# Order of the sync queue, the place of the mask bias, and the order on ScalarE in a graph-attention kernel

## The chip, the cores and the metric

The kernel runs on one core of one Trainium2 chip. The metric is the device time of one execution in microseconds (us), the median over the runs shown. One core has a matrix engine (TensorE, PE in the profile; its weight loads stand on a line of their own, PEld), three engines that work on tiles in on-chip memory (VectorE = DVE, ScalarE = ACT, GpSimd = POOL), and SyncE (SP), which here does nothing but start transfers between main memory and on-chip memory. Each engine runs its own list of instructions strictly in order. An instruction that waits for another engine or for a transfer holds up everything behind it on its own list; that includes SP, whose list is called the sync queue here.

## The reference

Sixteen sequences (B = 16) of N = 512 positions and F = 512 features; 16 heads; every position attends to the first 20 positions only, in two directions with their own weights. Cut to what matters:

```python
def _forward(v, q, adj, W_self, b_self, w_bias, b_bias, Wq, bq, Wk, bk, Wout, bout):
    row_zero = v.sum(-1) == 0
    q_exp = jnp.where(row_zero[..., None], 0.0, q[:, None, :])
    self_feat = jnp.concatenate([v, q_exp], axis=-1) @ W_self.T + b_self
    output = self_feat
    for d in range(2):
        A = adj_f if d == 0 else jnp.swapaxes(adj_f, 1, 2)
        A = A[:, :, :20, :]                       # (B, 512, 20, 11)
        cond, vb = A.sum(-1), A @ w_bias + b_bias
        # inside _gat_attention:
        aff = jnp.einsum('bnhd,bmhd->bnhm', qh, kh) / sqrt(dh)
        aff = jnp.where(cond[:, :, None, :] > 0, aff, -9e15) + vb[:, :, None, :]
        w = softmax(aff)                          # over the 20 keys
        output = output + einsum(w @ kv, Wout) + bout
    return v + relu(output)
```

Two details carry the change. `row_zero` is a flag for each position, and `q` is added only where the row's sum is not zero. `b_bias` is one number that is added to every attention score.

## The kernel before

**Setup.** Weights and key-side products that don't depend on the 512 query positions are made first: keys `g` (for each sequence a 128 x 4 x 608 tile; the first in `g0`, the second stored to `g1_d`, the others to `g_d`), the score terms from the biases `cq` (stored to `cq_d`, L524), values `vw` (stored to `vw_d`). In the main part values are read back in a block layout: `clear_blocks` (L123) writes zeros over all of `bd_d` (2 MB), `blocks` (L130) copies the values into it with 12 transfers, `load_values` (L115) loads one sequence's blocks into `vd` with four transfers.

**Main loops.** For each sequence b (16) there are four steps nt (tiles of 128 query positions). The order of all instructions is written out by hand: the scheduler is off (`manual_schedule`), so an engine's list is the order in which the Python calls are made. The names for each step:

- `store()` at the start of each step sends the finished output tiles to memory (256 KB each, four for each sequence). What `residual` (L337) has appended by then is sent.
- `load_adj(b, h)` the mask of half a sequence (440 KB, three buffers); `load_cq` four transfers; `load_x` (1 MB, four buffers); `load_xn` two halves of the sequence in another layout (512 KB each, one buffer for each half), which serve only the row sums; `load_keys` (1.2 MB, two buffers); `load_values` (four transfers, **one** buffer, so a new load must wait until `attend` of the sequence before has read the old one).
- `self_feat(b, f, h)` on TensorE (L186) makes half of the feature rows for half of the positions into a PSUM bank; `self_copy` (L194, the vector instruction at L199) adds `q` times the row flag `nz` and moves it to `sf`. For sequence b+1, `ahead` puts (f 0 and 1, h 0) into step 3 of sequence b, and (0, 1) and (1, 1) into its own steps 0 and 1.
- `scores` on TensorE (L253, 128 matmul instructions as the profile counts them) needs `sf` and the keys. `weigh` on VectorE (L267, L271, L273), `expo` on ScalarE (L278), `normal` (L304, L305 on VectorE, L306 on GpSimd) and `turn` (L313 on VectorE) make the softmax; `normal` and `turn` of a step stand one step later.
- `attend(b - 1)` on TensorE (L324) stands in step 2 of sequence b and writes four PSUM banks, which it shares with `self_feat` (`ps_acc` has four). `finish` (L333 on VectorE, the relus at L335 on ScalarE) takes them out.
- The mask: `mask_mul` casts the integers on ScalarE (L207) and multiplies by the weights on GpSimd (L208); `mask_count` (L213 on VectorE, L214 on GpSimd) adds the large negative number; `mask_sum` reduces (L219 on VectorE); `mask_spread` copies the result to the 128 partitions with 16 small instructions on ScalarE (L228), which also add `b_bias` (`bb_sb`); `full_add` (L242 on GpSimd) adds `cq`.

**The row flags.** `row_sum` (L149, ScalarE, four for each sequence) sums the rows of `xn`. `row_mask` (L151) turns the sums into flags on VectorE (L153) and sends 2 KB to memory (`nz_d`, L154). `load_nz` (L156) loads them back, spread over all partitions (`nz`, L158); it has to wait until the store has landed. For b = 0 and 1 the flags are made on chip in the setup; the other 14 sequences go through memory.

**The sync queue for one sequence before**, in order: [step 1] mask half 0 of b+1, `cq` of b+1; [step 2] values of b, keys of b+1, x of b+2, mask half 1 of b+1, both halves of `xn` of b+2, flags of b+1 to memory, flags of b+1 back; [steps 3 and 0] four outputs. For b = 0 the clearing and the 12 block copies stand in step 1, ahead of x(2) and of mask half (1, 1).

Of the kernel before, what the change touches and what calls it, by code (L numbers as in the profile page):

```python
# [9 lines left out]
AF = mybir.ActivationFunctionType  # L10
# [3 lines left out]
P = 128  # L14
# [4 lines left out]
def gat_kernel(  # L19
# [20 lines left out]
    nc = tc.nc  # L40
    B, F, N = xT.shape
# [5 lines left out]
    BM = B * NG  # L47
# [4 lines left out]
    R = P // HL  # L52
# [39 lines left out]
    def load_xn(b, h):  # L92
        t = xns[b, h] = load.tile([P, 2, F], F32, tag="xn", name=f"xn{b}_{h}")
        nc.sync.dma_start(t, xn[b].rearrange("(p j) f -> p j f", j=4)[:, 2 * h : 2 * h + 2])
# [15 lines left out]
    def load_keys(b):  # L110
        gs[b] = gp.tile([P, C, WD], F32, tag="g", name=f"g{b}")
        src = g1_d if b == 1 else g_d[:, :, b - 2]
        nc.sync.dma_start(gs[b].rearrange("p c (a w) -> p (c a) w", a=C), src.rearrange("x p w -> p x w"))

    def load_values(b):  # L115

        vds[b] = gp.tile([P, HL, 2, DH], F32, tag="vd", name=f"vd{b}", bufs=1)
        for c in range(C):
            nc.sync.dma_start(
                vds[b][bass.ts(c, 32)].rearrange("p e i g -> p (e i g)"), bd_d[c, b].rearrange("r e i g -> r (e i g)")  # L120
            )
# [8 lines left out]
    def blocks():  # L130

        bb = bd_d.rearrange("c b r e i g -> (c b) r e i g")
        vv = vw_d.rearrange("d c (b m) (e g) -> d (c b) m e g", m=NG, e=HL)
        for e in range(HL):
            for i in range(2):
                j = (e * S) // 32 + i
                for d in range(2):
                    lo = max(e * S + d * NG, 32 * j)
                    hi = min(e * S + (d + 1) * NG, 32 * j + 32)
                    if lo < hi:  # L140
                        m, r = lo - e * S - d * NG, lo - 32 * j
                        nc.sync.dma_start(bb[:, r : r + hi - lo, e, i], vv[d, :, m : m + hi - lo, e])  # L142
# [8 lines left out]
    def row_mask(b, queue=nc.sync):  # L151
        t = msk.tile([P, 4], F32, tag="nz4", name=f"nz4_{b}")
        nc.vector.tensor_scalar(t, rss[b], 0.0, None, ALU.not_equal)  # L153
        queue.dma_start(nz_d[b].rearrange("(p j) -> p j", j=4), t)  # L154

    def load_nz(b, queue=nc.sync):  # L156
        nzs[b] = load.tile([P, N], F32, tag="nz", name=f"nz{b}")
        queue.dma_start(nzs[b], nz_d[b : b + 1].partition_broadcast(P))  # L158
# [45 lines left out]
    def mask_mul(b, h):  # L204
        a = adjs[b, h]
        p = prods[b, h] = msk.tile([P, 2 * S, L + 1], F32, tag="prod", name=f"prod{b}_{h}", bufs=1)
        nc.scalar.copy(p[:, :, :L], a.rearrange("p t (m l) -> p (t m) l", l=L))  # L207
        nc.gpsimd.tensor_mul(p[:, :, :L], p[:, :, :L], wb_sb.unsqueeze(1).to_broadcast([P, 2 * S, L]))  # L208
# [13 lines left out]
    def mask_spread(b, h, quarters=range(4)):  # L222

        add = conds[b, h]
        for a in quarters:
            for g in range(HL):
                r = bass.ts(g, R)
                nc.scalar.activation(  # L228
                    adds[b, h][bass.ts(a, R), :, g], add[r].rearrange("p (t m) -> p t m", t=2),
                    AF.Identity, bias=bb_sb[r],  # L230
                )

    def mask_add(b, h):
        mask_sum(b, h)
        mask_spread(b, h)
# [111 lines left out]
    with tc.tile_pool(name="setup", bufs=1) as sp:  # L347
# [157 lines left out]
        with tc.tile_pool(name="setup_g", bufs=4) as sg:  # L505

            def bias_scores(d):

                ps = ps_acc.tile([P, 512], F32, tag="acc", name=f"ps_c{d}")
                for c in range(C):  # L510
                    nc.tensor.matmul(
                        ps[bass.ts(c, DH), : B * ND], bqbd[:, d, c], khD[:, d * C + c],
                        start=True, stop=True,
                    )
                if d == 0:
                    stages["c"] = load.tile([P, 2, F], F32, tag="xn", name="c")
                    nc.gpsimd.memset(stages["c"][:, :, :BM], 0.0)
                t = stages["c"][:, d, :BM]
                nc.scalar.copy(
                    t.rearrange("p (b m) -> p b m", m=NG)[:, :, 1:],  # L520
                    ps[:, : B * ND].rearrange("p (b m) -> p b m", m=ND),
                )
                for c in range(C):
                    nc.gpsimd.dma_start(  # L524
                        cq_d[:, bass.ts(c, HL), d].rearrange("b h m -> h b m"),
                        t[c * DH : c * DH + HL].rearrange("p (b m) -> p b m", m=NG),
                    )
# [130 lines left out]
    with tc.manual_schedule():  # L658
# [11 lines left out]
        for b in range(B):  # L670
# [13 lines left out]
            for nt in range(NT):  # L684
                store()
                if nt == 1:
                    if b + 1 < B:
                        load_adj(b + 1, 0)
                        load_cq(b + 1)
                    if b == 0:  # L690
                        clear_blocks(zero)
                        blocks()
                if nt == 3 and b == 0:
                    load_values(b)
                if nt == 2:
                    if b > 0:
                        load_values(b)
                    if 0 < b < B - 1:
                        load_keys(b + 1)
                    if b + 2 < B:  # L700
                        load_x(b + 2)
                    if b + 1 < B:
                        load_adj(b + 1, 1)
                    if b + 2 < B:
                        load_xn(b + 2, 0)
                        load_xn(b + 2, 1)

                if b == B - 1 and nt == 2:

# [2 lines left out]
                    mask_add(b, 1)  # L712
                if nt == 3 and b + 1 < B:
                    mask_add(b + 1, 0)
                if prev is not None and (nt != 2 or b == 0):
                    normal(*prev)
                final = b == B - 1 and nt == NT - 1
# [7 lines left out]
                if nt == 2 and b > 0:  # L725
                    banks = [ps_acc.tile([P, 512], F32, tag="acc", name=f"ps_o{b - 1}_{q}") for q in range(4)]
                    attend(b - 1, banks)
                    o = work.tile([P, C, N], F32, tag="o", name=f"o{b - 1}")
                    finish(b - 1, o, banks)
                    normal(*prev)  # L730
                    if b + 1 in rss:
                        row_mask(b + 1)
                        load_nz(b + 1)
                if final:

                    o_last = gp.tile([P, C, WD], F32, tag="g", name=f"o{b}")[:, :, :N]
# [10 lines left out]
                    mask_mul(b, 1)  # L747
                    mask_count(b, 1)
                if nt == 2 and b + 1 < B:
                    mask_mul(b + 1, 0)  # L750
                    mask_count(b + 1, 0)
                for part in ahead(nt):
                    self_copy(*part)
# [30 lines left out]
                if nt >= 2 and b > 0:  # L784
                    if not final:
                        residual(b - 1, 2 * nt - 4, o)
                    residual(b - 1, 2 * nt - 3, o)
                if 0 < b < B - 1 and nt < 2:
                    row_sum(b + 1, 2 * nt)
                    row_sum(b + 1, 2 * nt + 1)  # L790
                prev = (b, nt, s)
        store()
        b = B - 1
# [80 lines left out]
```

## Time and profile before

| | value |
|---|---|
| median of 3 runs (lowest, highest) | 663.02 us (661.27, 664.54) |
| the profiled execution, own time | 666.13 us |
| its span in the trace | 664.3 us |
| mean granted TensorE clock | 0.983 |
| PE busy | 627.7 us, 94% |
| PEld busy | 462.0 us, 70% |
| DVE busy | 468.4 us, 71% |
| ACT busy | 362.7 us, 55% |
| POOL busy | 370.7 us, 56% |
| share of the last-ending chain that is PE | 85% |
| moved by transfers | 124.17 MB, mean 187 GB/s |

A line of the profile names the engine, the source line, the operation, the tile written and the tiles read. Busy time is the time in which an engine worked, idle time is given with what ended it. The chain of waits is followed back from the last instruction: at each step to what released it, or to the instruction before it on the same engine. "issue" is time in which an engine waited for nothing that the profile names. The granted clock is the share of the full TensorE clock.

### The profile page before, as it was taken

The page shows a single profiled execution, that of the slowest core. Times are in us where ns is not written, and L with a number is a line of the kernel's source. Part 1 is how long each engine was busy: PE and PEld are TensorE (multiplying, and loading weights), DVE is VectorE, ACT ScalarE, POOL GpSimd, SP SyncE. Part 2 cuts the span into 40 slices and gives each one's busy share as a digit, 9 for nine tenths or more (in the row PEclk, how much of TensorE's full clock was granted, in tenths as well). Part 3 has the DMA queues.
Part 4 walks back from the last instruction along what each step waited for, and adds up shares of the span by engine and source line. Part 5 has one row for each costly group of instructions (what it writes and reads, how often), then busy time and mean ns, then how long its engine had stood idle before and what let it go on. Part 6 is the DMA issues. An engine that isn't in the chain of part 4 may idle for free.

```text
span 664.3 us, 31036 instructions
## 1 busy us (share of the span) xinstructions
PE 627.7 (94%) x13932; PEld 462.0 (70%) x13932; DVE 468.4 (71%) x754; ACT 362.7 (55%) x862; POOL 370.7 (56%) x301
## 2 busy tenths in 40 slices
PE   9999999989989999898989899999989898999995
PEld 6654468847767768776777686686767677777883
DVE  1576658484949596785949494968768585949786
ACT  1335626274755647373847466473737384747671
POOL 3307225256574756565555757466655655575785
PEclk9999999979999999998999999999999999999998
DMA  8999997837171727364362717273736446362403
GB/s 302 389 381 312 368 326 212 238 95 263 30 275 56 263 87 239 114 221 133 110 244 72 249 42 273 75 242 112 238 116 209 146 145 209 85 243 57 150 29 127
DMA packets 97684, 124.17 MB, mean 187 GB/s; under 512 B 19504, under 2 KB 69712, under 8 KB 95504
## 3 DMA queue, kind: packets, MB, share of 16 engines
q1 hardware_dynamic: 96304, 120.31, 53.3%
q8 instruction: 109, 1.79, 1.1%
q0 software_dynamic: 672, 1.36, 0.9%
q10 hardware_dynamic: 576, 0.53, 0.3%
q14 instruction: 23, 0.19, 0.1%
HBM read 82.30 MB, written 40.24 MB: 184 GB/s over the span
## 4 chain that ended last, share of the span: by engine, by line
PE 85%; issue 5%; DMA 3%; DVE 3%; SPq 3%; ACT 0%; POOL 0%; DVEq 0%; POOLq 0%; ACTq 0%
PE ps_s L253 37%; PE ps_sf L186 30%; PE ps_o L324 7%; PE ps_v L537 3%; PE ps_k L475 3%; PE ps_kv L426 2%; SPq L142 2%; DMA bd_d<-zero 1%; DMA adj<-in_adj 1%; DMA g_d<-st 1%; PE ps_warm L385 1%; SPq L98 0%; DVE ps_s L271 0%; DVE wt L313 0%; DVE o L333 0%
## 5 line engine op out<-in xcount | busy, mean ns | idle before, releaser
L253 PE MATMUL ps_s<-g,sf 128*32 128x152 f32 x8192 | 286.8, 297 | 22.0 <-issue 21.5
L253 PEld LDWEIGHTS ps_s<-g,sf 128*32 128x32 f32 x8192 | 261.6, 111 | 57.2 <-issue 41.7
L186 PE MATMUL ps_sf<-x,ws_v 128*32 128x236 f32 (+1 forms) x4096 | 225.5, 371 | 1.8 <-issue 1.8
L228 ACT ACTIVATE both<-add,bb_sb 32x80 f32<-32x80 f32 x512 | 183.2, 358 | 42.6 <-DVE add L219 36.5
L186 PEld LDWEIGHTS ps_sf<-x,ws_v 128*32 128x32 f32 x4096 | 138.5, 110 | 72.0 <-issue 6.5
L242 POOL TENSOR_TENSOR full<-cq,both 128x640 f32<-128x640 f32 x64 | 99.9, 1562 | 92.5 <-ACT both L228 61.0
L278 ACT ACTIVATE s<-s 128x640 f32<-128x640 f32 x63 | 46.5, 738 | 180.6 <-DVE s L273 178.3
L306 POOL TENSOR_TENSOR s<-s,sm 128x640 f32<-128x640 f32 x63 | 80.2, 1273 | 109.3 <-DVE sm L305 94.8
L199 DVE SCALAR_TENSOR_TENSOR sf<-nz,qw,ps_sf 128x236 f32<-128x236 f32 (+1 forms) x128 | 51.3, 452 | 102.4 <-DMA nz<-nz_d 101.2
L208 POOL TENSOR_TENSOR prod<-prod,wb_sb 128x880 f32<-128x880 f32 x32 | 67.6, 2113 | 29.0 <-ACT prod L207 29.0
L338 POOL TENSOR_TENSOR o<-o,x 128x512 f32<-128x512 f32 x60 | 75.3, 1276 | 0.0
L267 DVE TENSOR_TENSOR full<-ps_s,full 128x608 f32<-128x608 f32 x63 | 49.4, 784 | 13.5 <-PE ps_s L253 7.2
L324 PE MATMUL ps_o<-wt,vd 32*32 32x512 f32 (+2 forms) x1088 | 50.7, 597 | 6.3 <-DVE wt L298 1.9
L271 DVE TENSOR_REDUCE ps_s<-full 128x32 f32<-128x640 f32 x63 | 52.2, 828 | 2.2
L273 DVE TENSOR_TENSOR s<-full,ps_s 128x640 f32<-128x640 f32 x63 | 51.7, 821 | 2.2
L313 DVE STREAM_TRANSPOSE wt<-s 128x640 f32<-128x640 f32 x63 | 52.7, 837 | 0.1
L304 DVE TENSOR_REDUCE sm<-s 128x32 f32<-128x640 f32 x63 | 51.0, 809 | 1.8
L219 DVE TENSOR_REDUCE add<-prod 128x80 f32<-128x960 f32 x32 | 36.2, 1132 | 18.9 <-POOL prod L214 18.8
L335 ACT ACTIVATE o<-o,bo 128x512 f32<-128x512 f32 x60 | 38.2, 707 | 0.0
L213 DVE TENSOR_REDUCE cond<-adj 128x80 f32<-128x880 int32 x32 | 33.2, 1038 | 6.8 <-DMA adj<-in_adj 6.8
L333 DVE TENSOR_TENSOR o<-ps_o,sf 128x512 f32<-128x512 f32 x60 | 36.7, 670 | 0.9 <-PE ps_o L324 0.9
L324 PEld LDWEIGHTS ps_o<-wt,vd 32*32 32x32 f32 x1088 | 15.8, 104 | 30.1 <-issue 20.7
(212 smaller groups left out, 408.1 us busy)
## 6 DMA issues: line engine op xcount, KB each, us to landing
g<-g_d SPq DMA_DIRECT2D x15, 1216.0 KB, 7.2
g_d<-st SPq DMA_DIRECT2D x16, 1064.0 KB, 6.5
x<-in_xT SPq DMA_DIRECT2D x16, 1024.0 KB, 9.3
out_T<-o SPq DMA_DIRECT2D x60, 256.0 KB, 3.1
xn<-in_xn SPq DMA_DIRECT2D x28, 512.0 KB, 9.1
adj<-in_adj SPq DMA_DIRECT2D x32, 440.0 KB, 7.8
nz<-nz_d SPq DMA_DIRECT2D x14, 256.0 KB, 3.5
wk<-in_wkT SPq DMA_DIRECT2D x2, 1024.0 KB, 8.0
```

Of the source, the lines that this page charges most:

```text
L186: nc.tensor.matmul(held[0][bass.ts(a, R), i * N // 2 : i * N // 2 + hi - lo], ws_v[:, k, bass.ds((2 * f + i) * P + a * R, R)], xs[b][:, k, ...
L199: nc.vector.scalar_tensor_tensor(sfs[b][:, 2 * f + i, lo:hi], nzs[b][:, lo:hi], qw[:, 2 * f + i, b : b + 1], ps[:, i * N // 2 : i * N // 2 ...
L208: nc.gpsimd.tensor_mul(p[:, :, :L], p[:, :, :L], wb_sb.unsqueeze(1).to_broadcast([P, 2 * S, L]))
L228: nc.scalar.activation(adds[b, h][bass.ts(a, R), :, g], add[r].rearrange("p (t m) -> p t m", t=2), AF.Identity, bias=bb_sb[r],)
L242: nc.gpsimd.tensor_add(f, cqs[b].unsqueeze(1).to_broadcast(shape), adds[b, nt // 2][:, nt % 2].unsqueeze(2).to_broadcast(shape),)
L253: nc.tensor.matmul(bank[bass.ts(a, R), bass.ts(j, WD // HL)], sfs[b][:, k, bass.ds(nt * P + (2 * g + j) * R, R)], keys[:, k, a], start=(k ...
L271: nc.vector.tensor_reduce(mx, f, AX.X, ALU.max)
L273: nc.vector.tensor_sub(s, f, mx.unsqueeze(3).to_broadcast(full))
L306: nc.gpsimd.tensor_mul(s, s, sm.unsqueeze(3).to_broadcast(full))
L313: nc.vector.transpose(wts[b][:, nt], s.rearrange("p a h m -> p (a h m)"))
L324: nc.tensor.matmul(banks[a][bass.ts(e, DH)].rearrange("p (t n) -> p t n", n=32), vds[b][r, e, i], wt[r, :, bass.ts(j, 32)], start=start an ...
L338: nc.gpsimd.tensor_add(o[:, c], o[:, c], xs[b][:, c])
```

## The change

Five edits.

1. `load_values(b)` moves from step 2 to step 3 (it stays in step 2 for the last sequence).
2. The four row sums of b+1 all stand in step 0 (before: two in step 0, two in step 1). `row_mask(b+1)` moves from step 2 to the end of step 1, and `load_nz(b+1)` to the head of step 2 on the sync queue, ahead of keys, x, mask half 1 and `xn`.
3. For b = 0, mask half (1, 1) goes ahead of x(2), and the 12 block copies go behind x(2) and both halves of `xn`(2).
4. `b_bias` is added once to the score terms before they are stored to `cq_d` (two new vector instructions on GpSimd in the setup); the 16 spreading instructions become plain copies.
5. `mask_mul(b+1, 0)` is called at the head of step 2: its cast stands ahead of the four relus on ScalarE, its product ahead of `normal`'s product on GpSimd.

```diff
@@ mask_spread
-                nc.scalar.activation(
-                    adds[b, h][bass.ts(a, R), :, g], add[r].rearrange("p (t m) -> p t m", t=2),
-                    AF.Identity, bias=bb_sb[r],
-                )
+                nc.scalar.copy(adds[b, h][bass.ts(a, R), :, g], add[r].rearrange("p (t m) -> p t m", t=2))
@@ bias_scores
+                nc.gpsimd.tensor_add(t, t, bb_sb.to_broadcast([P, BM]))
@@ main loop
                     if b == 0:
                         clear_blocks(zero)
-                        blocks()
-                if nt == 3 and b == 0:
-                    load_values(b)
                 if nt == 2:
-                    if b > 0:
-                        load_values(b)
+                    if b + 1 in rss and b > 0:
+                        load_nz(b + 1)
                     if 0 < b < B - 1:
                         load_keys(b + 1)
+                    if b == 0:
+                        load_adj(1, 1)
                     if b + 2 < B:
                         load_x(b + 2)
-                    if b + 1 < B:
+                    if 0 < b < B - 1:
                         load_adj(b + 1, 1)
                     if b + 2 < B:
                         load_xn(b + 2, 0)
                         load_xn(b + 2, 1)
+                    if b == 0:
+                        blocks()
+                if nt == (3 if b + 1 < B else 2):
+                    load_values(b)
...
+                if nt == 2 and b + 1 < B:
+                    mask_mul(b + 1, 0)
                 if prev is not None and (nt != 2 or b == 0):
                     normal(*prev)
...
-                    if b + 1 in rss:
-                        row_mask(b + 1)
-                        load_nz(b + 1)
...
                 if nt == 2 and b + 1 < B:
-                    mask_mul(b + 1, 0)
                     mask_count(b + 1, 0)
...
-                if 0 < b < B - 1 and nt < 2:
-                    row_sum(b + 1, 2 * nt)
-                    row_sum(b + 1, 2 * nt + 1)
+                if 0 < b < B - 1:
+                    if nt == 0:
+                        for j in range(4):
+                            row_sum(b + 1, j)
+                    if nt == 1:
+                        row_mask(b + 1)
```

## The prediction

> **What bounds the kernel now.** I read the page first: the last-ending chain is 85% TensorE, so TensorE's work sets the time, and the question is where TensorE stands still. The chain of waits in order of time shows a repeating period, from one `attend` (L324) to the next. TensorE's timeline inside one of them (columns: start us, length us, line, operation, count, in brackets the idle time before it):
>
> ```profile
> 445.96 3.64 PE L186 MATMUL ps_sf<-x,ws_v 128*32 128x256 f32 x64
> 451.11 4.63 PE L253 MATMUL ps_s<-g,sf 128*32 128x152 f32 x128 [1.52 <-issue]
> 455.56 3.64 PE L186 MATMUL ps_sf<-x,ws_v 128*32 128x256 f32 x64
> 459.01 4.32 PE L253 MATMUL ps_s<-g,sf 128*32 128x152 f32 x128
> ```
>
> Before the scores of a sequence's step 0 TensorE stands 1.52 us, and these scores take 0.3 us more than the next. "issue" names no cause; VectorE's timeline does:
>
> ```profile
> 443.30 0.35 DVE L305 RECIPROCAL sm<-sm 128x32 f32<-128x32 f32 x1
> 450.55 1.57 DVE L199 SCALAR_TENSOR_TENSOR sf<-nz,qw,ps_sf 128x236 f32<-128x236 f32 x4 [6.90 <-DMA nz<-nz_d]
> ```
>
> VectorE stands 6.9 us for the row flags; TensorE starts 0.6 us after L199 begins, because these scores read `sf`. Why the flags are late stands on the sync queue:
>
> ```profile
> 431.47 1.70 SPq L119 DMA_DIRECT2D vd<-bd_d  x4
> 433.21 0.42 SPq L113 DMA_DIRECT2D g<-g_d  x1
> 433.68 2.15 SPq L90 DMA_DIRECT2D x<-in_xT  x1
> 435.94 0.84 SPq L98 DMA_DIRECT2D adj<-in_adj  x1
> 436.88 0.90 SPq L94 DMA_DIRECT2D xn<-in_xn  x2
> 437.87 0.38 SPq L154 DMA_DIRECT2D nz_d<-nz  x1
> 446.93 0.33 SPq L158 DMA_DIRECT2D nz<-nz_d  x1
> ```
>
> The 2 KB of flags go out behind 3.7 MB of keys, x, mask and xn, and land 9 us later; only then may they be loaded back. The values ahead of all this wait for `attend`. The table of waits gives the totals (us in total, times, longest):
>
> ```profile
> SPq L119 <- PE ps_o L324: 168.0, 15, 13.0
> SPq L158 <- DMA nz_d<-nz: 116.1, 14, 9.8
> ```
>
> One period serves as an experiment in the trace: at b = 14 no x and no xn are left to load. The flags are stored at 613.74, loaded at 620.60, VectorE waits 2.10 us only, and TensorE never stops:
>
> ```profile
> 609.36 4.34 PE L253 MATMUL ps_s<-g,sf 128*32 128x152 f32 x128
> ...
> 624.02 3.64 PE L186 MATMUL ps_sf<-x,ws_v 128*32 128x256 f32 x64
> 627.47 4.32 PE L253 MATMUL ps_s<-g,sf 128*32 128x152 f32 x128
> 631.61 3.64 PE L186 MATMUL ps_sf<-x,ws_v 128*32 128x256 f32 x64
> 635.06 4.32 PE L253 MATMUL ps_s<-g,sf 128*32 128x152 f32 x128
> 639.31 2.35 PE L324 MATMUL ps_o<-wt,vd 32*32 32x512 f32 x64
> 641.59 8.47 PE L253 MATMUL ps_s<-g,sf 128*32 128x152 f32 x256
> ```
>
> From the end of one `attend` to the end of the next: 641.59 - 609.36 = 32.23 us. That is a period without any stall. `attend` takes 2.35 us here and 3.45 at 605.97, where its fourth matmul waits for a PSUM bank that L199 at 606.26 empties. So a late VectorE costs a second time, 1.1 us.
>
> **Part 1, the flags and the queue (edits 1 and 2).** The first `attend` starts at 135.27, the fourteenth (b = 14) at 606.04: 470.77 us for 13 periods, 36.21 each, 3.98 over 32.23. If every stall goes: 13 x 3.98 = 51.8 us. Whether it goes I work out by placing all the work of a period against an unstopped TensorE (0 = `attend` starts; scores end at 0, 6.5, 17.1, 24.7, 32.2; the feature rows at 12.9, 20.5, 28.1), durations from the rows of VectorE's, ScalarE's and GpSimd's timelines.
> - *VectorE*: `weigh` 0 to 2.4, `turn` to 3.2, the flags (0.1) 3.3, `finish` 5.7, `normal` to 6.8, mask count to 7.8, `weigh` to 10.2, `turn` 11.0, mask sum 12.0, `normal` 13.1, L199 four times 13.1 to 14.6, idle to 17.1, `weigh`, `turn`, `normal`, count, L199 twice to 23.2, idle to 24.7, `weigh`, `turn`, sum, `normal`, L199 twice to 30.7, idle to 32.2. It idles 5.5 of 32.2 us. The bank that `attend` wants is empty at 30.7, 1.5 us early, so the second cost goes too.
> - *ScalarE*: all four row sums (4 x 0.8 us) now follow `expo` of step 0 and end at 31.0, that is at -1.2. Queued behind them are the 16 spreads (5.9 us as now, to 4.7) and `expo` (to 5.4), which `normal` at 5.7 needs; `full_add` on GpSimd (1.57) ends at 6.3, and VectorE reads it at 7.8. They fit by 0.3 and 1.5 us.
> - *The sync queue*: the flags' store is issued at 3.3 + 0.4. What came ahead of it (two outputs, mask half 0, `cq`) was issued around -10 to -7.6 and has landed, so it meets empty queues. No row shows it in that state: the flag transfers lie between 3.1 and 10.5 us to landing. I take 3.1, since another store to memory, 256 KB of output, has a median of 3.1. SP stands until 6.9, the load back lands after 0.3 + 3.5 at 10.7. VectorE wants it at 13.1; TensorE is touched only when L199 ends after 20.5, so with a landing after 19.0. Even the slowest, 10.5, gives 18.1.
> - *Behind this wait on SP* stand keys, x, mask half 1 and both xn. Keys are issued at 7.2, land 7.2 later (page, median) at 14.8 with their issue, and are wanted at 20.5. Mask half 1 landed 10.5 us after the keys' issue in the period shown (435.94 + 7.8 - 433.21), so at 17.7; ScalarE wants it at 20.2, VectorE at 21.4. xn is wanted at 27.8. The values, now behind two outputs that GpSimd finishes at 14.4, take 4 issues and about 2 us and are wanted at 32.2.
>
> The row sets the cost of the two-way trip. The Trainium skill, "DMA: Bandwidth & Descriptors", section "Rules for kernel authors", says to issue a transfer early and to wait for it late; this change does the reverse on SP, which waits with 3.7 MB behind it. The trace agrees that such a wait delays what is behind it (the values' wait above), but the spare 5.7 us of the keys pay for it; read strictly, the rule would cost what the slowest store does, 1.7 us a period on the keys, or 22 us in all.
>
> **The clock.** In four of the 13 periods the granted clock dipped, in three of them at a gap of 2.03 to 2.20 us and once at the stop around 134 to 138. Two windows (us, PE, PEld, DVE, ACT, POOL busy, then PEclk, share of the transfer engines, GB/s):
>
> ```profile
> 195.88:206.00 10.12, 8.03 (x169) 6.02 (x172) 8.34 (x15) 1.56 (x2) 5.29 (x5) 0.83 0.49 163
> 445.00:456.00 11.00, 9.48 (x238) 7.06 (x234) 5.27 (x9) 5.00 (x13) 5.70 (x5) 1.00 0.50 167
> ```
>
> A gap of 2.09 us has 0.83, one of 1.52 has 1.00. The dip is already in the 3.98, and I take it to go with the gap. The skill's "TensorE: Matmul & The Clock Gate", Part 1, puts the drop after an idle window of about 3.4 us; by that, gaps of 2.09 us would not be the cause and the four dips might stay. Their size from the trace: scores took 6.06, 6.07 and 5.99 instead of 4.63, and one `attend` 1.7 more, about 6 us, which by the page alone would come back.
>
> **Part 2, the start (edit 3).** Before, mask half (1, 1) was issued at 122.38, behind the clear's landing (8.6) and 12 block issues (10.64); VectorE waited for it until 130.2, and TensorE stood 1.39 and 1.76 us around 134 to 138. After, it is issued at about 101.6 and lands with the clear ahead of it (landed at 109.8, then 0.44 MB at 302 GB/s, the lowest of the page's first four slices) near 111; it is wanted after 123. The first `attend` starts at 133.9 instead of 135.27: 1.4 us; what it lost inside is in the 51.8. The blocks now queue behind x and xn. Kindly they end as before, at 124; harshly they start when x and xn have landed too (2.5 MB at 302 GB/s after 109.8: 118) and take 10.6 + 3.5 + 2 + 2 to the values, 136.1, which is 2.2 after 133.9. I take half, -1.1, and keep 0 and -2.2.
>
> **Part 3, the bias (edit 4).** A copy of 80 elements for each partition takes 0.258 us (L182), the spreading instruction 0.358: 512 x 0.1 = 51 us of ScalarE's 363 busy us go, 1.6 in each spread. By the placing above, that widens ScalarE's 0.3 us to 1.9 and moves no end of TensorE, so it counts zero. Without that cover a spread would hold `normal` by its whole delay. The two additions cost GpSimd between 0.56 (L214, 80 elements) and 1.27 (L163, 512) each, 0.8 by size, in a stretch where TensorE is busy for all of 46 us; `cq` is wanted 25 us later. Zero, at worst 2.5.
>
> **Part 4, the cast (edit 5).** On ScalarE 0.92 us ahead of the relus, on GpSimd 2.11 ahead of `normal`'s product: that product ends at 9.7, VectorE wants it at 10.2. In return mask sum no longer waits (1.59 us a period for L214, on VectorE). Hidden: zero; if the cover is gone at most 0.92 a period, 12 us.
>
> **The tail.** From 606.04 on only the `attend` there gains, 1.1.
>
> **Sum.** 664.3 - 51.8 - 1.4 + 1.1 - 1.1 = 611.1 us of span. The execution's own time is 1.8 above its span: 612.9; the median shown (663.02) is 3.1 below this execution (666.13). So about 610 us.
>
> **The rivals.**
> - *The second cost stays*: `attend` still waits for its bank, because ScalarE's bunched row sums make VectorE late. For it: the margin of 0.3 us. Against: edit 4 gives 1.6, and 639.31 shows no wait. 13 x 1.1 = 14: 624 us. Chance 0.12.
> - *A new wait for keys or mask half 1*: the round trip holds them past 20.5. For it: SP's wait and the 10.5 row. Against: 5.7 us spare. With 1 to 3 us a period, say 2: 26 more, 636 us. Chance 0.08.
> - *It does not do what it says*: the flags arrive early, but another wait keeps the old pace. Against: the b = 14 period, which has the same engines and runs in 32.23. About 663. Chance 0.02.
> - *Slower*: SP's stand for the flags' store. It decides from the point where the keys' lateness exceeds today's loss of 3.98 us a period: spare 5.7 + 3.98 + the 3.1 assumed, a landing of 12.8 us. The worst row is 10.5, with far more traffic ahead. At 15 us: 13 x 2.2 = 29 over today, 692. Chance 0.04.
>
> **How the numbers follow.** The forecast has 0.74, its own range 605 to 619 (the clock's 6, the setup's 2.5, scatter of the runs). The range reaches through the second cost and partly to the third case, 604 to 630. Faster by over 0.5%, which is about what a measurement of this kernel can tell from no change: 0.74 + 0.12 + 0.08 = 0.94; within 0.5%: 0.02; slower: 0.04.
>
> **What would show it.** Right: VectorE's wait for `nz` gone from the table or under 10 us; flags to memory landing in 3 to 5 us; periods of 32.2 to 32.6; `attend` at 2.35 throughout; the clock at 1.00 after the first sequence; ScalarE's busy time down by some 50 us without effect on the end. Wrong: "DMA g" or "DMA adj" as releaser of TensorE, VectorE or ScalarE; a stall before the first `attend` released by `vd`; SP waiting over 9 us for the flags' store.

## The result, and the profile after

| | before | after |
|---|---|---|
| median, us (lowest, highest; 4 runs each, on one chip) | 663.78 (661.27, 669.12) | 624.50 (623.73, 625.46) |
| profiled execution, own time / span | 666.13 / 664.3 | 623.73 / 621.9 |
| first `attend` starts | 135.27 | 133.38 |
| fourteenth `attend` starts | 605.97 | 564.29 |
| mean period between them | 36.21 | 33.15 |
| mean granted clock | 0.983 | 0.995 |

The ratio is 0.9399, with an interval of 0.9339 to 0.9459. Two more measurements of the changed kernel, in the groups of runs below, gave 627.64 us (0.9438, interval 0.9409 to 0.9467) and 627.62 us (0.9446, 0.9412 to 0.9480). The forecast was about 610, with 605 to 619 for its own case and 604 to 630 with the rivals.

The profiled spans differ by 42.4 us, and the table says where: 1.9 ahead of the first `attend`, 13 x 3.06 = 39.8 in the thirteen periods, 0.7 behind them. Of the 39.8, 6.0 lie in the first period (38.81 before, 32.80 after), in which the first `attend` took 6.91 us before and takes 2.35 now. Of the 1.9, 1.3 lie ahead of the first key product (17.05 before, 15.78 after), in the loads of the weights, which the change leaves alone. (Line numbers after are three lower: L250 scores, L321 `attend`, L264 the first step of `weigh`, L335 `residual`; L199 and L186 have stayed.) The page's shares of the chain that ended last, after:

```profile
PE 95%; DVE 3%; issue 1%; ACT 0%; POOL 0%; DVEq 0%; POOLq 0%; ACTq 0%
```

TensorE had 85% of it before. The sync queue's timeline in one period after:

```profile
302.17 0.34 SPq L154 DMA_DIRECT2D nz_d<-nz  x1
303.63 0.34 SPq L158 DMA_DIRECT2D nz<-nz_d  x1
304.06 0.39 SPq L113 DMA_DIRECT2D g<-g_d  x1
304.50 5.14 SPq L90 DMA_DIRECT2D x<-in_xT  x1
309.73 0.96 SPq L98 DMA_DIRECT2D adj<-in_adj  x1
310.79 0.90 SPq L94 DMA_DIRECT2D xn<-in_xn  x2
```

The flags go out first and the load back is issued 1.5 us later; before it was 9.1. VectorE's timeline where it stood for 6.9 us before:

```profile
310.69 0.81 DVE L301 TENSOR_REDUCE sm<-s 128x32 f32<-128x640 f32 x1
311.53 0.35 DVE L302 RECIPROCAL sm<-sm 128x32 f32<-128x32 f32 x1
311.80 1.47 DVE L199 SCALAR_TENSOR_TENSOR sf<-nz,qw,ps_sf 128x236 f32<-128x236 f32 x4
```

L199 follows without a wait. In the table of all waits no line with `nz` as releaser of VectorE is left (101.2 us before); SP's own wait for the flags' store has shrunk from 116.1 us (us in total, times, longest):

```profile
SPq L158 <- DMA nz_d<-nz: 23.7, 14, 2.6
```

What is left on TensorE, in its timeline of the same period:

```profile
310.66 4.32 PE L250 MATMUL ps_s<-g,sf 128*32 128x152 f32 x128
314.79 1.47 PE L186 MATMUL ps_sf<-x,ws_v 128*32 128x256 f32 x23
316.62 2.54 PE L186 MATMUL ps_sf<-x,ws_v 128*32 128x256 f32 x41 [0.35 <-issue]
318.80 3.06 PE L250 MATMUL ps_s<-g,sf 128*32 128x152 f32 x87
322.47 1.61 PE L250 MATMUL ps_s<-g,sf 128*32 128x152 f32 x41 [0.60 <-issue]
323.79 3.74 PE L186 MATMUL ps_sf<-x,ws_v 128*32 128x256 f32 x64
327.24 4.42 PE L250 MATMUL ps_s<-g,sf 128*32 128x152 f32 x128
```

The long stop ahead of the scores is gone. What is left are short stops *inside* a run of matmuls, after the 23rd of 64 and the 87th of 128, where no semaphore stands. They are not new. The kernel before had five of them in its main loops, at 156.93, 299.14, 410.70, 481.92 and 553.28, hidden among the long ones. The second of them in its chain of waits (start us, length us, what):

```profile
296.30 2.84 PE ps_s L253 x87
299.14 0.81 issue
299.95 1.58 PE ps_s L253 x41
```

With what they do to the matmuls beside them, such stops are most of what the forecast missed.

What they are can be read from the records of transfers. The page's queue "q8 instruction" has 109 packets of 16 KB; TensorE has some 28,000 records in a run (matmuls, weight loads and waits), so a packet is about 256 of its instructions. Counting TensorE's records from the start, every stop between 130 and 600 us in the changed kernel lies at the same place of such a block of 256 (start us, length us, record number modulo 256, time since the last of these packets ended):

```
155.24 0.13  193  1.51      388.42 0.51  194  1.59
189.97 0.12  194  1.41      419.42 0.37  193  1.43
220.46 0.22  193  1.52      449.20 0.03  193  1.26
286.37 0.40  193  1.27      454.76 0.88  194  1.25
316.26 0.35  193  1.46      486.24 0.39  193  1.49
321.87 0.60  194  1.36      515.79 0.19  193  1.25
352.94 0.18  193  1.36      521.53 0.58  194  1.49
382.85 0.19  193  1.49
```

So TensorE runs out of instructions, and goes on 1.25 to 1.6 us after the next 16 KB have come. The idle time in these 15 stops is 5.2 us, but the matmuls beside them are slower too. Set start by start against the periods of 32.23 us that four of the runs below contain, the thirteen periods of the changed kernel lose 11.9 us, and 11.0 of it falls near these places, from 6 matmuls ahead of each to 14 behind it.

Each stretch from one of these places to the next is called a block from here on. Two of the fetches, in the summaries of the transfers in two such blocks of the changed kernel (the row is the busy share of the transfer engines in 40 slices, in tenths; then the queue, packets, MB, share). First the block that ends with the stop at 316.26:

```profile
DMA  8999799999999999999999999999999999694997
...
q8 instruction: 1, 0.02, 1.2%
```

Then a block in a quiet stretch, 331.69 to 336.5:

```profile
DMA  0000040000000000000000000000000000000000
...
q8 instruction: 1, 0.02, 1.2%
```

In the quiet one the only packet is the fetch, in the sixth slice, 0.7 us after the block began. In the busy one it started 2.85 us after, while x, mask and xn were on their way. Over the 93 blocks of the changed kernel that begin between 130 and 600 us: where the transfer engines are under 25% busy over the block, a fetch starts 0.28 us after its block begins (median of 38), where they are over 90% busy 2.63 us (median of 25). Every one of the 15 stops follows a fetch that started 2.5 us or more after its block began; the latest, 4.21 us, belongs to the longest stop, 0.88 us at 454.76. No fetch that started earlier is followed by a stop.

### The profile page after: what moved, and what is told of

It reads as the page before. It is cut to its first block, busy times and chain, and to the rows that moved or that the text cites. A ratio compares the mean times of both kernels' runs of the same rounds, so it can differ in the third digit from the quotient of the medians.

```text
span 621.9 us, 30998 instructions
## 1 busy us (share of the span) xinstructions
PE 607.3 (98%) x13932; PEld 468.4 (75%) x13932; DVE 478.3 (77%) x754; ACT 312.0 (50%) x862; POOL 374.1 (60%) x303
## 4 chain that ended last, share of the span: by engine, by line
PE 95%; DVE 3%; issue 1%; ACT 0%; POOL 0%; DVEq 0%; POOLq 0%; ACTq 0%
PE ps_s L250 42%; PE ps_sf L186 35%; PE ps_o L321 5%; PE ps_v L535 3%; PE ps_k L472 3%; PE ps_kv L423 1%; PE ps_warm L382 1%; DVE o L330 0%; PE ps_nz L169 0%; DVE wt L310 0%; DVE ps_s L268 0%; DVE sm L301 0%; DVE full L264 0%; POOL s L303 0%; PE ps_c L508 0%
## 5 line engine op out<-in xcount | busy, mean ns | idle before, releaser
L250 PE MATMUL ps_s<-g,sf 128*32 128x152 f32 x8192 | 285.6, 293 | 4.9 <-issue 4.1
L250 PEld LDWEIGHTS ps_s<-g,sf 128*32 128x32 f32 x8192 | 267.2, 110 | 28.3 <-issue 20.6
L186 PE MATMUL ps_sf<-x,ws_v 128*32 128x236 f32 (+1 forms) x4096 | 228.7, 371 | 1.6 <-issue 1.5
L186 PEld LDWEIGHTS ps_sf<-x,ws_v 128*32 128x32 f32 x4096 | 145.9, 110 | 66.5 <-issue 7.0
L228 ACT COPY both<-add 32x80 f32<-32x80 f32 x512 | 130.7, 255 | 22.1 <-DVE add L219 16.5
L264 DVE TENSOR_TENSOR full<-ps_s,full 128x608 f32<-128x608 f32 x63 | 49.6, 787 | 89.4 <-PE ps_s L250 75.3
L335 POOL TENSOR_TENSOR o<-o,x 128x512 f32<-128x512 f32 x60 | 75.9, 1286 | 0.0
L199 DVE SCALAR_TENSOR_TENSOR sf<-nz,qw,ps_sf 128x236 f32<-128x236 f32 (+1 forms) x128 | 50.0, 441 | 1.2 <-PE ps_sf L186 1.1
L321 PE MATMUL ps_o<-wt,vd 32*32 32x512 f32 (+2 forms) x1088 | 38.7, 582 | 2.1 <-DVE wt L295 1.9
L149 ACT ACTIVATE xn<-xn 128x512 f32<-128x512 f32 x56 | 34.4, 615 | 0.0
```

The lines of the kernel that those rows point to most:

```text
L186: nc.tensor.matmul(held[0][bass.ts(a, R), i * N // 2 : i * N // 2 + hi - lo], ws_v[:, k, bass.ds((2 * f + i) * P + a * R, R)], xs[b][:, k, ...
L228: nc.scalar.copy(adds[b, h][bass.ts(a, R), :, g], add[r].rearrange("p (t m) -> p t m", t=2))
L250: nc.tensor.matmul(bank[bass.ts(a, R), bass.ts(j, WD // HL)], sfs[b][:, k, bass.ds(nt * P + (2 * g + j) * R, R)], keys[:, k, a], start=(k ...
L321: nc.tensor.matmul(banks[a][bass.ts(e, DH)].rearrange("p (t n) -> p t n", n=32), vds[b][r, e, i], wt[r, :, bass.ts(j, 32)], start=start an ...
L335: nc.gpsimd.tensor_add(o[:, c], o[:, c], xs[b][:, c])
```

## The experiments

Three theories stood beside each other: the flags' place on the sync queue as the one cause of the long stop; the values' wait for `attend`, at the head of that queue, as the cause; and, for the 0.9 us a period that were left, the instruction fetches against anything on VectorE or ScalarE. Mean periods below are from the first to the fourteenth `attend` of the profiled execution.

**The flags alone (edit 2 on the kernel before).**

```diff
                 if nt == 2:
+                    if b + 1 in rss and b > 0:
+                        load_nz(b + 1)
                     if b > 0:
                         load_values(b)
...
-                    if b + 1 in rss:
-                        row_mask(b + 1)
-                        load_nz(b + 1)
...
-                if 0 < b < B - 1 and nt < 2:
-                    row_sum(b + 1, 2 * nt)
-                    row_sum(b + 1, 2 * nt + 1)
+                if 0 < b < B - 1:
+                    if nt == 0:
+                        for j in range(4):
+                            row_sum(b + 1, j)
+                    if nt == 1:
+                        row_mask(b + 1)
```

> The kernel before with edit 2 alone: the four row sums in step 0, the flags stored at the end of step 1 and loaded back at the head of step 2; the values stay in step 2, behind the flags, and the start stays as before. Theory (the flags' place on the sync queue is the loss): periods between two attends fall from 36.2 to the 33.1 us of the changed kernel, the wait of VectorE for nz is gone, and only the old start is lost against the changed kernel: its first attend began 1.8 us later and cost 4.6 us more, so 624.5 + 6.4 = about 631 us. Rival (the values' wait for attend at the head of the queue is the loss, the flags only show it): periods stay above 35 us, 655 us or more. Rival (the edits on ScalarE, 4 and 5, are needed, or attend waits for its PSUM bank again): 13 x 1.1 us more, about 645 us, with attend at 3.4 us instead of 2.35.

629.08 us (ratio 0.9478, 0.9418 to 0.9539), mean period 33.21, and no wait of VectorE for `nz`. The flags' place is enough, and neither of the two edits on ScalarE is needed for it.

**The values alone (edit 1 on the kernel before).**

```diff
-                if nt == 3 and b == 0:
-                    load_values(b)
                 if nt == 2:
-                    if b > 0:
-                        load_values(b)
...
+                if nt == (3 if b + 1 < B else 2):
+                    load_values(b)
```

> The kernel before with edit 1 alone: the values are loaded in step 3; the flags still go out behind keys, x, mask half 1 and xn. Theory: without the values' wait for attend at the head, keys, x, mask and the first xn half are issued some 8 us before attend instead of 2 us after its end, so they have landed when the flags are stored near 7 us after attend's start; the flags then land in about 3 us, come back near 13 to 14 us and are wanted at 13.1, while TensorE is touched only after 19. So this edit alone cures the periods too (33 to 33.5 us), and the time is 631 us as with the flags alone; what is not needed twice does not add up. Rival (the place of the flags decides, the values' wait does not matter): VectorE still waits 6 to 7 us a period for nz, periods stay near 36 us, 660 us.

628.33 us (0.9472, 0.9417 to 0.9527), mean period 33.56. The sync queue's timeline in one period of this run:

```profile
262.20 1.43 SPq L113 DMA_DIRECT2D g<-g_d  x1
263.67 1.66 SPq L90 DMA_DIRECT2D x<-in_xT  x1
265.44 1.03 SPq L98 DMA_DIRECT2D adj<-in_adj  x1
266.96 8.17 SPq L94 DMA_DIRECT2D xn<-in_xn  x2
276.74 0.33 SPq L154 DMA_DIRECT2D nz_d<-nz  x1
279.69 0.33 SPq L158 DMA_DIRECT2D nz<-nz_d  x1
```

The flags still go out last, but keys, x, mask and the first half of xn were issued 10 to 15 us ahead of them; the load back follows 2.95 us after the store. VectorE no longer waits for `nz`. In five of the later periods `attend` still takes 2.65 to 4.02 us here instead of 2.35; three of these hold a late fetch, and what else they lose was not traced. Both edits cure the same wait, and either does it alone. The cause before was the two together: a wait at the head of the queue that bunched the loads, and the flags behind the bunch.

**The old start (the change without edit 3).**

```diff
                         clear_blocks(zero)
+                        blocks()
...
-                    if b == 0:
-                        load_adj(1, 1)
                     if b + 2 < B:
                         load_x(b + 2)
-                    if 0 < b < B - 1:
+                    if b + 1 < B:
                         load_adj(b + 1, 1)
...
-                    if b == 0:
-                        blocks()
```

> The changed kernel without edit 3: the twelve block copies ahead of x(2) and mask half (1, 1) again. Theory: only the start changes; mask half (1, 1) lands at 130 again, the first attend begins 1.8 us later and costs 4.6 us more than 2.3: 624.5 + 6.4 = about 631 us, periods from the second on as in the changed kernel. Rival (the periods' gain hides the start, since the first sequence only shifts what comes after): 624 to 626 us.

631.0 us, beside 627.64 of the changed kernel: 3.4 us by the medians, with runs of 627.38 to 633.91 against 625.40 to 629.62, and 7.0 by the two profiled spans. The intervals of the two ratios overlap (0.9447 to 0.9514, and 0.9409 to 0.9467), so the profile has to decide. TensorE's timeline of this run around its first `attend`:

```profile
135.10 1.12 PE L321 MATMUL ps_o<-wt,vd 32*32 32x512 f32 x6 [1.87 <-DVE wt L310]
137.98 3.56 PE L321 MATMUL ps_o<-wt,vd 32*32 32x512 f32 x58 [1.76 <-issue]
```

The two stops of the kernel before are back; the first period is 38.3 us against 32.6 beside it. In all ten profiles with edit 3 the first `attend` takes 2.35 us, in the four without it 4.28 to 6.91. So the start is worth some 3 to 7 us, near the 6.4 expected.

**The bias as before (the change without edit 4).**

```diff
-                nc.scalar.copy(adds[b, h][bass.ts(a, R), :, g], add[r].rearrange("p (t m) -> p t m", t=2))
+                nc.scalar.activation(
+                    adds[b, h][bass.ts(a, R), :, g], add[r].rearrange("p (t m) -> p t m", t=2),
+                    AF.Identity, bias=bb_sb[r],
+                )
...
-                nc.gpsimd.tensor_add(t, t, bb_sb.to_broadcast([P, BM]))
```

> The changed kernel without edit 4: the 16 spreading instructions add the bias again (0.36 instead of 0.26 us each), and the two additions in the setup are gone. Theory: ScalarE's busy time rises by 52 us to about 364, the margin ahead of normal shrinks from 1.9 to 0.3 us, TensorE does not notice: within 0.5% of the changed kernel, 622 to 627 us. Rival (with the bunched row sums ScalarE makes normal late, VectorE gets late, attend waits for its PSUM bank): 13 x up to 1.1 us, 630 to 639 us, attend above 3 us.

624.27 us (0.9387, 0.9361 to 0.9413), 3.4 below the changed kernel beside it, mean period 33.14 against 33.12. ScalarE's groups of this run (operation, count, busy us, mean ns):

```profile
L228 ACT ACTIVATE both<-add,bb_sb 32x80 f32<-32x80 f32 x512 | 183.6, 359 | 22.0 <-DVE add L219 16.0
```

In the changed kernel the same 512 take 130.7 us, 255 ns each: 53 us of ScalarE's time, and TensorE's periods don't show them. The edit has a price in the setup instead. From the first key product to the first scores, the nine profiled executions of kernels with the two additions took 74.75 to 75.46 us, four of kernels without them 74.29 to 74.30. That is some 0.5 us; the other 3 us between the medians are not explained by it. The last run below takes this up.

**The cast as before (the change without edit 5).**

```diff
-                if nt == 2 and b + 1 < B:
-                    mask_mul(b + 1, 0)
...
                 if nt == 2 and b + 1 < B:
+                    mask_mul(b + 1, 0)
                     mask_count(b + 1, 0)
```

> The changed kernel without edit 5: the cast behind the four relus again, the product behind normal's product. Theory: VectorE's wait for the product at L219 is back, about 1.6 us a period, inside VectorE's idle time of 5.5 us: within 0.5%, 622 to 627 us. Rival (that wait pushes L199 and the bank that attend wants, or the scores of step 0): 1 us a period, 637 us.

627.63 us (0.9435, 0.9408 to 0.9461) beside 627.64. No difference. The wait for the product that was expected back came once in the run, 1.9 us, as it does in the changed kernel, and not in each period: VectorE, no longer late, reaches that place after the product.

**The changed kernel, the measure for these three.**

> The changed kernel once more, as the measure for the three runs beside it: 624 to 626 us, periods of 33.1 us, first attend near 133.5.

627.64 us, 1.6 above the expected range; mean period 33.12; the first `attend` at 135.39, 2 us later than in the first profile, most of it in the loads of the weights: the first key product starts at 17.42 here, at 15.78 there.

**One MB more in the burst.**

```diff
                         load_xn(b + 2, 0)
                         load_xn(b + 2, 1)
+                        if b > 0:
+                            for h in range(2):
+                                t = work.tile([P, 2, F], F32, tag="more", name=f"more{b}_{h}")
+                                nc.sync.dma_start(t, xn[b].rearrange("(p j) f -> p j f", j=4)[:, 2 * h : 2 * h + 2])
```

> The changed kernel with one more MB loaded in each sequence behind the two xn halves, into a tile that nobody reads. The 0.9 us a period that the changed kernel lies above 32.23 us. Theory (TensorE's own instructions come in 16 KB fetches over the same transfer engines; a fetch in the middle of the 3.7 MB burst comes late, and TensorE runs dry): the burst lasts some 2.5 us longer, another fetch falls into it, and the loss grows to between 1.3 and 2.2 us a period: 630 to 642 us, with every gap of TensorE 1.2 to 1.7 us after the end of a fetch. Rival (the 0.9 us come from VectorE or from a semaphore, not from the transfers): 624 to 626 us, gaps as before.

636.42 us (0.9599, 0.9552 to 0.9646, above all three measurements of the changed kernel), mean period 33.90. 21 stops, 13.2 us in all, against 15 and 5.2, each at record 193 or 194 of a block, 1.2 to 1.6 us after a fetch. TensorE's timeline at the longest of them:

```profile
257.32 3.17 PE L250 MATMUL ps_s<-g,sf 128*32 128x152 f32 x88
262.61 0.60 PE L250 MATMUL ps_s<-g,sf 128*32 128x152 f32 x12 [2.12 <-issue]
```

**The burst taken apart on the sync queue.**

```diff
-                    if b + 2 < B:
+                    if b == 0:
                         load_x(b + 2)
...
-                    if b + 2 < B:
+                    if b == 0:
                         load_xn(b + 2, 0)
                         load_xn(b + 2, 1)
...
                     load_values(b)
+                if nt == 3 and 0 < b and b + 2 < B:
+                    load_xn(b + 2, 0)
+                    load_xn(b + 2, 1)
+                if nt == 0 and 1 < b < B - 1:
+                    load_x(b + 1)
```

> The changed kernel with the burst taken apart: keys and mask half 1 stay in step 2, xn goes to step 3 behind the values, x to step 0 of the next sequence behind two outputs (one sequence ahead instead of two). The same bytes in all. Theory (late instruction fetches in the burst): the bursts hold 1.9, 1.0 and 1.4 MB instead of 3.7, fetches come in time, the period falls from 33.15 to 32.3 to 32.6 us, 615 to 619 us. Rival (the loss is not from the burst): 624 to 626 us. Rival (a moved load now comes late: x is wanted 14 us after its issue, xn 8 us): slower than 626, with DMA x or DMA xn as releaser of TensorE or ScalarE.

624.87 us (0.9427, 0.9375 to 0.9478), mean period 32.94: a miss. The ratio lies among the three of the changed kernel (0.9399, 0.9438, 0.9446); none of these was measured beside this run. Its periods alternate, 32.2 and 33.3 to 34.5. The chain of waits in one of the long ones (start us, length us, what):

```profile
188.29 3.10 PE ps_s L250 x96
191.39 0.22 issue
191.61 1.24 PE ps_s L250 x32
192.85 3.45 PE ps_sf L186 x64
196.30 1.03 PE ps_s L250 x32
197.33 0.92 issue
198.25 3.31 PE ps_s L250 x96
```

The stops are still fetches (record 193 or 194), but they have moved: from the keys' burst to the new one of x, outputs and mask half 0 in steps 0 and 1. A period has 1664 matmuls and weight loads, 6.5 blocks, so the fetches fall half a block further on in every second period; that fits the alternation, and was not tested by itself.

**Without the loads of x and xn.**

```diff
-                    if b + 2 < B:
+                    if b == 0:
                         load_x(b + 2)
+                    elif b + 2 < B:
+                        xs[b + 2] = xs[2]
...
-                    if b + 2 < B:
+                    if b == 0:
                         load_xn(b + 2, 0)
                         load_xn(b + 2, 1)
+                    elif b + 2 < B:
+                        xns[b + 2, 0], xns[b + 2, 1] = xns[2, 0], xns[2, 1]
```

> The changed kernel without the loads of x and xn from the fourth sequence on; TensorE and ScalarE work on the third sequence's tiles again, so the loads are left out and the outputs of those sequences are not the reference's. Same instructions on TensorE, 2 MB less in each burst (1.9 MB left). Theory (TensorE's instruction fetches come late in the burst): most of the 0.9 us a period goes, periods 32.2 to 32.6, 613 to 618 us, gaps of TensorE almost gone. Rival (the fetches are late for another reason, or the loss is VectorE's): 624 to 627 us as the changed kernel beside it.

616.54 us (0.9271, 0.9226 to 0.9315), mean period 32.45, against 33.26 of the changed kernel beside it; of its 18 stops 2 are left, 0.5 us together. The same instructions on TensorE with 2 MB less beside them in each period: 0.8 us a period come from the traffic.

**The transfers set apart, on two queues.** This kernel leaves nothing out.

```diff
+    def load_x_half(b, h):
+        if h == 0:
+            xs[b] = load.tile([P, C, N], F32, tag="x", name=f"x{b}", bufs=4)
+        cs = slice(2 * h, 2 * h + 2)
+        nc.scalar.dma_start(xs[b][:, cs], xT[b].rearrange("(c p) n -> p c n", p=P)[:, cs])
...
-                    if b + 2 < B:
+                    if b == 0:
                         load_x(b + 2)
-                    if 0 < b < B - 1:
-                        load_adj(b + 1, 1)
-                    if b + 2 < B:
                         load_xn(b + 2, 0)
                         load_xn(b + 2, 1)
...
+                if nt == 3 and 0 < b < B - 1:
+                    load_adj(b + 1, 1)
...
                     expo(s)
+                    if nt == 3 and 0 < b and b + 2 < B:
+                        load_x_half(b + 2, 0)
+                    if nt == 0 and 1 < b < B - 1:
+                        load_x_half(b + 1, 1)
...
                             row_sum(b + 1, j)
+                            if j % 2 and b + 2 < B:
+                                load_xn(b + 2, j // 2, nc.scalar)
```

> The changed kernel with its transfers set apart in time: xn from ScalarE's own queue behind the row sums, x in two halves from ScalarE's queue behind the exponentials of steps 3 and 0, mask half 1 in step 3; flags and keys alone stay in step 2. No burst holds more than 1.5 MB. Theory (a fetch is late only when a burst outlasts the 2.7 us that it may be late): periods 32.2 to 32.6, 614 to 619 us, faster than the changed kernel beside it. Rival from the run that took the burst apart on the sync queue alone (its periods were 32.2 and 33.6 in turn, 32.94 in the mean): a fetch then meets another burst, 32.9, no gain, 624 to 627. Rival (ScalarE is held up by the issues and makes normal late): slower than the changed kernel.

618.25 us (0.9298, 0.9267 to 0.9329), 9.4 us below the changed kernel beside it, mean period 32.64. The busy share of the transfer engines in 40 slices, from the page of the changed kernel:

```profile
DMA  8999999719282646546381909182735556382503
```

And from the page of this run:

```profile
DMA  8999999855666556566474746576655465653503
```

The same bytes, but 9 beside 1 has become 5 beside 6. TensorE's timeline of one period of this run:

```profile
298.19 2.35 PE L327 MATMUL ps_o<-wt,vd 32*32 32x512 f32 x64
300.48 4.34 PE L256 MATMUL ps_s<-g,sf 128*32 128x152 f32 x128
304.63 6.56 PE L192 MATMUL ps_sf<-x,ws_v 128*32 128x236 f32 x128
311.01 4.32 PE L256 MATMUL ps_s<-g,sf 128*32 128x152 f32 x128
315.14 3.64 PE L192 MATMUL ps_sf<-x,ws_v 128*32 128x256 f32 x64
318.59 4.32 PE L256 MATMUL ps_s<-g,sf 128*32 128x152 f32 x128
322.73 3.64 PE L192 MATMUL ps_sf<-x,ws_v 128*32 128x256 f32 x64
326.18 4.32 PE L256 MATMUL ps_s<-g,sf 128*32 128x152 f32 x128
```

No idle time in brackets; 3 stops between 130 and 600 us, 2.2 us together. Seven of the thirteen periods last 32.2 to 32.3 us; most of the others hold such a late fetch or an `attend` of 2.5 to 3.0 us, whose cause stays open. The Trainium skill, "DMA: Bandwidth & Descriptors", section "Issuing engines are not separate DMA queues", says that issuing from several engines saves only issue time. On bandwidth this run says nothing against it; here the second queue serves to start transfers at other moments. How much of the 9.4 us is due to the queue and how much to the new moments, the run does not tell apart.

**The changed kernel, the measure for these two.**

> The changed kernel as the measure for the two runs beside it: 624 to 628 us, periods 33.1.

627.62 us, mean period 33.26, 18 stops, 6.1 us.

**The same with the bias as before (without edit 4).** The diff is that of the bias run above, on the kernel with the transfers set apart.

> The run with the transfers on ScalarE's queue, with edit 4 undone (bias added in the spreading, no additions in the setup). In every profile so far the kernels with edit 4 need 74.7 to 75.5 us from the first key product to the first scores, those without it 74.3. Theory: 0.5 us less in the setup, nothing else: 616 to 619 us. Rival (undoing edit 4 was worth the 3 us by which that run lay below the changed kernel beside it): 614 to 615 us. Rival (ScalarE now also issues transfers, and with the dearer spreads it makes normal late): 621 us or more.

617.17 us (0.9289, 0.9253 to 0.9325), not to be told from 618.25 (0.9298). From the first key product to the first scores it takes 74.30 us, as the other four without the additions. So the 3 us of the bias run were not the price of edit 4; what is shown of that edit is its 0.5 us in the setup.

## Why the prediction was right, and where not

**The cause and the size class: right.** The late flags held VectorE and through L199 TensorE; with the flags in time the wait is gone, and 39.8 of the 42.4 us lie in the periods, 6.0 of them in the first one, where the old start was. The flags alone (edit 2) bring the mean period to 33.21, the values alone to 33.56. The measured 624.5 us lies inside 604 to 630 partly by luck: the forecast's own case, 605 to 619, was missed, and the upper part of the range stood there for other losses than the one that came.

**The placing of a period: right, with small differences.** The flags' store landed in 2.1 us (median; taken: 3.1), the load back in 4.4 (taken: 3.5). The 3.1 was read from the stores and loads of the flags together; the stores alone took 6.8 to 10.5 before. The flags' own instruction on VectorE (L153) takes 0.91 us at its new place (taken: 0.1), inside VectorE's idle time. `attend` takes 2.35 us in all sequences but the last, which has a form of its own, so its second wait, the first rival, is gone. Neither TensorE nor VectorE waits for keys, mask or xn in the main loops.

**The step that failed: 13 x 3.98 = 51.8, "if every stall goes".** It measured 13 x 3.06 = 39.8, and the periods came down to 33.15 us, not to 32.2 to 32.6. The 3.98 us were put down to the late flags as a whole, though the trace before already had five stops of the other kind. The 32.23 us of an unstopped period came from b = 14, and that period runs smoothly for two reasons: its flags are in time, and x and xn are not loaded in it. The forecast used the missing traffic as evidence for the first and overlooked that TensorE's own instructions travel beside it. There was luck in the 32.23 too: the same period of the changed kernel, also without x and xn, takes 32.72 us (32.75 and 32.88 in its two later profiles). With the traffic away (32.45) or spread (32.64) the period comes near to 32.23; with more of it, it moves away (33.90). The 624 us of the first rival were met by the measured time, but not by its mechanism.

**The start: near.** The blocks behind x and xn did not delay the first `attend` in the first profile (133.38 without a wait in front); the forecast had taken 1.1 for it. What the edit brings lies inside the first `attend` and in the stop ahead of it, not in its starting time, which moves by as much with the loads of the weights (133.38, 135.39 and 136.88 in the three profiles of the changed kernel). Edit 3 is worth 3.4 us by the medians and 7.0 by the spans, against the 6.4 expected before its run.

**Edits 4 and 5: zero was taken.** Edit 5 measured zero. Edit 4 cost 0.5 us in the setup, within the bounds of 0 to 2.5; its saving on ScalarE is real and hidden.

**The wait on SP with the loads behind it.** The rule to issue early and wait late did not bite: SP waited 1.7 us on average for the store, 2.6 at most, and what came behind it was in time.

**The clock.** The dips went with the stops (the granted clock is 1.00 from 90 to 564 us, 0.995 over the whole span). So the four dips did not stay, as they might have by the 3.4 us of the page that the prediction names; here the measurement decides. But a stop's length does not settle it: before, stops of 2.03, 2.09 and 2.20 us had dips (0.83 over some 10 us), one of 2.00 at 268.05 had none, and the run with one MB more had one of 2.12 without a dip. The Trainium skill, "TensorE: Matmul & The Clock Gate", Part 1, tells of a window that runs freely and does not reset when a kernel starts. That would fit stops of one length with and without a dip, and no run here tests it.

## What to carry to other kernels

Look at what a small transfer has ahead of it on its queue, and at what holds the head of the queue: 2 KB of flags took 9.3 us behind 3.7 MB and 2.1 us ahead of it, and curing either the order or the wait at the head was enough to end VectorE's wait. A stretch of the trace that serves as the ideal must carry the same load as the rest; here the "unstopped" period lacked the very traffic that costs the others most of 0.9 us. When TensorE is 98% busy and still stops inside a run of matmuls, compare the place with the instruction fetches, and spread the transfers over the period.

## What was not expected of the hardware

TensorE's instruction fetches, 16 KB for about 256 instructions, share the transfer engines with the data and come late in a burst: 2.63 us (median) instead of 0.28 after their block began, when the engines are over 90% busy instead of under 25%. At 128 matmuls, with as many weight loads, in 4.1 to 4.3 us a block is used up before the next is there, and TensorE goes on 1.2 to 1.6 us after the fetch has ended. Whether the fetch waits for the transfer engines or for the memory behind them, these runs do not separate. The same bytes more evenly spread were worth 9.4 us of 627.6.
